# A chunk's gate, output projection and residual addition one slot later in a pipelined Mamba-2 and mixture-of-experts block

## The chip, the core and the metric

The kernel runs on one core of a Trainium2 chip. Its time is the device time of one execution in microseconds. Five engines with queues of their own work side by side: PE (matrix products; its weight loads are listed as PEld), DVE, ACT and POOL (elementwise work), and SP, which here only issues DMAs. Each queue runs in order, so an instruction that waits holds up all that stand behind it on its engine.

## The reference

Eight sequences of 512 tokens with 128 features go through a modulated layer norm, four Mamba-2 layers with a residual, a gated residual, and a mixture of eight experts (two per token) with a shared expert. The change lies in the Mamba layers. The reference steps through the tokens one by one; cut to what matters:

```
for l in range(4):
    zxbcdt = rmsnorm(h) @ Wi                      # z, xBC, dt
    xBC = silu(conv4(xBC)); xs, Bm, Cm = split(xBC)
    dt  = softplus(dt + dtb); dA = exp(-dt * exp(Alog))
    hs  = hs * dA_t + (dt_t * xs_t) B_t           # per token t, per head
    y_t = hs . C_t + D * xs_t
    h   = h + rmsnorm(y * silu(z), gw) @ Wo
```

## The kernel before

The recurrence is done in chunks of 128 tokens. A unit is one sequence in one layer; there are 32 units (u), of four chunks each, so 128 chunks, called items (i). Two units form a group, whose running sums are made together. Everything is float32.

One Python loop (L993) runs over slots t, and each slot takes a different stage of several items, so that the stages form a software pipeline. The context manual_schedule keeps the written order on every engine. The order in a slot sets the order of the queues; what makes an engine wait is data or a buffer. For the code, p = t + 16 is the slot of the projections, whose units are four ahead.

In a slot t, in this order:

- ACT takes the exponent of item t+1's decay matrix dV (decay_exp, L809).
- PE makes item t's part from the state and the state's increment (state_out, L861 and L870, into a bank py) and item t-1's output (chunk_out, L910 and L920, into its py).
- POOL scales the state (state_decay, L886) and weighs the transposed input (weigh, L836 and L839).
- In every fourth slot ACT does silu of z and of the convolution's output (L672, L673), into a tile sz for z.
- DVE multiplies dV by the Gram matrix (mix, L852), in even slots adds the finished pair of items t-4 and t-3 into the residual (out_add, L967), and finishes the state (state_next, L895 and L902; for a first chunk ACT copies it, L900).
- DVE multiplies item t-1's output by silu(z) (gate, L932) and ACT squares it (square, L936).
- PE makes the group's running sums in every eighth slot (sums_a, L748 to L750), then projects item t-2 (project_out: L947 sums the squares, L951 is the product with Wo). Two items share one bank po, in which an even one starts a new tile.
- PE makes item t+1's Gram matrix (gram, L848) and item t+2's transposes (L828), which ACT copies to xT (L830). Both go into one bank, ptx, the only one of its pool.
- POOL subtracts and masks item t+2's decay (L793, L798). DVE does three convolution taps (L660) and, between them in odd slots, the scale of the pair (out_scale: L958 on DVE, the power at L959 on POOL).
- The generators of gens take one step each. renorm, one per unit, normalizes a finished unit for the next layer: squares on ACT (L155), a power on POOL (L150), scaling on ACT (hn, L203), a slot with nothing, transposes on PE and the copy hT on ACT (L208, L210). At the end of the stage rejoin does the same for the mixture's input.
- PE projects dt (L682), DVE does one piece of softplus (L706 to L740), DVE and ACT copy out the running sums (sums_b, L756 to L763), SP writes them to DRAM as crow (L765) and POOL makes dtd (L767) of them. PE projects one part of x (px, L638) and ACT starts its convolution (L650); in every fourth slot PE projects z (pz, L644). SP loads item t+4's decay rows from crow into dV (L779).

The parts of a slot recur after eight slots. With r = t modulo 8: sums_a and sums_b are in r3; silu is in r1 and r5, z in r0 and r4; renorm starts in r3 and r7 and ends four slots later, in the slot in which the next one starts.

The pools that matter: psY (py, two banks), psO (po, two), psX (ptx, one), psP (all other products, three banks), eight in all; szp (sz, four tiles, L576); wk (g and sq, two each). scale_weights (L604, L605) puts four operations on POOL at the head of one slot r4 in 32 slots.

Of the kernel before, what the change touches and what calls it, by code (L numbers as in the profile page):

```python
# [13 lines left out]
PSUM = bass.MemoryType.PSUM  # L14
# [6 lines left out]
LEAD = 4  # L21
# [3 lines left out]
def adaln_mamba_moe(  # L25
# [28 lines left out]
    B, L, DM = x.shape  # L54
# [4 lines left out]
    NC = L // Q  # L59
# [445 lines left out]
    def pbank(name):  # L505
        return psP.tile([P, 512], F32, tag="p", name=name)
# [66 lines left out]
    with ExitStack() as actx:  # L573
# [7 lines left out]
        df = actx.enter_context(tc.tile_pool(name="df", bufs=6))  # L581
        rows = actx.enter_context(tc.tile_pool(name="rows", bufs=3, space=bass.MemoryType.DRAM))
        psX = actx.enter_context(tc.tile_pool(name="psX", bufs=1, space=PSUM))
        psY = actx.enter_context(tc.tile_pool(name="psY", bufs=2, space=PSUM))
        psO = actx.enter_context(tc.tile_pool(name="psO", bufs=2, space=PSUM))

        U = NL * B
        NI = U * NC
# [6 lines left out]
        def load_weights(l):  # L595
            Wi[l] = wip.tile([P, NPROJ], F32, tag="Wi", name=f"Wi{l}")
            nc.sync.dma_start(Wi[l], W_in[l])
            Wo[l] = wp.tile([P, NB, DM], F32, tag="Wo", name=f"Wo{l}")
            nc.sync.dma_start(Wo[l], W_out[l].rearrange("(k p) m -> p k m", p=P))
# [27 lines left out]
        def renorm(u):  # L627

            l, b = divmod(u, B)
            yield from rms_transposed(b, 1e-5, bw[:, l + 1 : l + 2], f"_{u}", pbank, htp, NC - 2)  # L630
            hT[u + B] = hTs.pop(b)
# [8 lines left out]
        def project_z(v):  # L640
            l = v // B
            for k in range(NB):
                pz[v, k] = pbank(f"pz{v}_{k}")
                nc.tensor.matmul(pz[v, k][:, :L], Wi[l][:, k * P : (k + 1) * P], hT[v], start=True, stop=True)  # L644
# [124 lines left out]
        def where(i):  # L769

            u, s = divmod(i, NC)
            g, bi = divmod(u, GROUP)
            return u, s, g, bi * n + s * NH
# [37 lines left out]
        def item_slice(i):  # L811
            s = i % NC
            return slice(s * Q, (s + 1) * Q)
# [115 lines left out]
        def gate(i):  # L929
            u, s, g, h0 = where(i)  # L930
            gs[i] = wk.tile([P, NB, Q], F32, tag="g", name=f"g{i}")
            nc.vector.tensor_mul(gs[i], py.pop(i)[:, :NB, :], sz[u][:, :, item_slice(i)])  # L932

        def square(i):
            sqs[i] = wk.tile([P, NB, Q], F32, tag="sq", name=f"sq{i}")
            nc.scalar.activation(sqs[i], gs[i], AF.Square)  # L936


        def project_out(i):
            l = i // NC // B  # L940
            g, sq = gs.pop(i), sqs.pop(i)
            c = i % 2
            if c == 0:
                po[i // 2] = psO.tile([P, 512], F32, tag="o", name=f"po{i}")
            pp = po[i // 2]
            for k in range(NB):
                nc.tensor.matmul(  # L947
                    pp[:, 2 * DM + c : 2 * DM + c + 1], sq[:, k, :], ones[:, 0:1], start=(k == 0), stop=(k == NB - 1)
                )
            for k in range(NB):  # L950
                nc.tensor.matmul(  # L951
                    pp[:, c * DM : (c + 1) * DM], g[:, k, :], Wo[l][:, k, :], start=(k == 0), stop=(k == NB - 1)
                )

        def out_scale(i):
            if i % 2:
                rs = small.tile([P, 2], F32, tag="rg", name=f"rg{i}")
                nc.vector.tensor_scalar(rs, po[i // 2][:, 2 * DM : 2 * DM + 2], 1.0 / DI, 1e-5, ALU.mult, ALU.add)  # L958
                nc.gpsimd.tensor_tensor(rs, rs, mhalf[:, 0:2], ALU.pow)  # L959
                po[i // 2] = po[i // 2], rs  # L960

        def out_add(i):
            if i % 2:
                pp, rs = po.pop(i // 2)
                for c in range(2):
                    b, s = i // NC % B, i % NC - 1 + c
                    nc.vector.scalar_tensor_tensor(  # L967
                        hs[b][:, s, :], pp[:, c * DM : (c + 1) * DM], rs[:, c : c + 1], hs[b][:, s, :], ALU.mult, ALU.add
                    )

        def item(i):
            return 0 <= i < NI

        def unit(v):
            return 0 <= v < U

        def group_stages(p, stages):

            for stage, late in stages:
                q, r = divmod(p - late, NC)  # L980
                if r == 0 and unit(q) and q % GROUP == GROUP - 1:
                    stage(q // GROUP)

        actx.enter_context(tc.manual_schedule())
        gens = {}
# [4 lines left out]
                    del gens[key]  # L990

        EARLY = 9
        for t in range(-NC * LEAD - EARLY, NI + 4):  # L993
            p = t + NC * LEAD
            drain = p >= NI
            if p == 5 - EARLY:
                gens["small"] = load_small()
            if p == 0:
                gens["experts"] = prepare_experts(df)
            if p == 7 - EARLY:  # L1000
                gens["lists"] = clear_lists()
            if t == NI - LEAD * NC + 2:
                for k, w in enumerate((sw1, sw2.rearrange("(k p) o -> p k o", p=P))):
                    w12.append(wip.tile([P, NPROJ], F32, tag="Wi", name=f"ws{k}")[:, :FH])
                    dst = w12[k] if k == 0 else w12[k].rearrange("p (k o) -> p k o", o=DM)
                    nc.sync.dma_start(dst, w)
            for g, seqs in enumerate(sets):
                if t == NC * (U - B) + NC * (seqs[-1] + 1) + 2:
                    gens["pairs", g] = rejoin(g)
            v, j = divmod(p, NC)  # L1010
            vc, jc = divmod(p - 1, NC)

            if (p + 2 * NC) % (NC * B) == 0 and unit(p // NC + 2):
                load_weights((p // NC + 2) // B)
            if p % (NC * B) == NC and unit(v):
                scale_weights(v // B)
            if p == NC:
                nc.scalar.activation(negA, negA, AF.Exp)
                nc.scalar.mul(negA, negA, -1.0)
            if (p + EARLY) % NC == 0 and 0 <= (p + EARLY) // NC < B:  # L1020
                gens[(p + EARLY) // NC] = enter((p + EARLY) // NC)
            if t % NC == 3 and unit(t // NC - 1) and t // NC - 1 + B < U:
                gens[t // NC - 1 + B] = renorm(t // NC - 1)

            if item(t + 1):
                decay_exp(t + 1)

            if item(t):
                state_out(t)
            if item(t - 1):  # L1030
                chunk_out(t - 1)
            if item(t):
                state_decay(t)
            if item(t + 1):
                weigh(t + 1)
            if drain and scatters and item(t + 2):
                scatter(*scatters.pop(0)[1:])
            vz, jz = divmod(p - 5, NC)
            if jz == 0 and unit(vz):
                silu(vz)  # L1040
            if item(t):
                mix(t)
            if item(t - 3):
                out_add(t - 3)
            if item(t):
                state_next(t)
            if drain:
                step_pairs()
            if item(t - 1):
                gate(t - 1)  # L1050
                square(t - 1)
            group_stages(p, ((sums_a, 7),))
            if item(t - 2):
                project_out(t - 2)
            if item(t + 1):
                gram(t + 1)
            if item(t + 2):
                transposes(t + 2)
            if item(t + 2):
                decay_diff(t + 2)  # L1060
                decay_mask(t + 2)
            if unit(vc):
                conv_tap(vc, jc, 1)
            if item(t - 2):
                out_scale(t - 2)
            if unit(vc):
                conv_tap(vc, jc, 2)
                conv_tap(vc, jc, 3)
                px.pop((vc, jc))
            for key in list(gens):  # L1070
                if not step(gens[key]):
                    del gens[key]
            if drain and routed:
                serve()
            if j == 1 and unit(v):
                project_dt(v)
            group_stages(p, ((softplus_a, 2), (softplus_b, 3), (softplus_c, 5), (softplus_d, 6), (sums_b, 7)))
            if unit(v):
                project_x(v, j)
                conv_first(v, j)  # L1080
            if j == 0 and unit(v - 1):
                project_z(v - 1)
            if item(t + 4):
                decay_rows(t + 4)

# [244 lines left out]
```

## Time and profile before

| | us |
|---|---|
| median of 3 runs (lowest, highest) | 1151.76 (1150.76, 1159.22) |
| the profiled execution, its span | 1149.48, 1147.8 |
| PE busy | 967.3 (84%) |
| DVE busy | 855.8 (75%) |
| ACT busy | 763.3 (67%) |
| POOL busy | 856.6 (75%) |
| first and last mix (L852) | 88.35, 859.67 |
| mean granted PE clock | 0.925 |

The page's second part cuts the span into 40 slices and gives the busy tenths of each:

```profile
PE   2767899889999999999988999979564994999985
DVE  2768888798888978988879889988754652666653
ACT  3686889789798788787978988776624741333320
POOL 6877979789798897887988988889766163555550
```

One character is 28.7 us. The even middle, characters 4 to 27, is the pipelined stage of the Mamba layers; then come its end with the routing, and the experts, where PE is at nine tenths. The change touches the stage up to about 880 us alone.

Busy time is an engine's own account; a wait is told by who ended it. "ACT sq L936 <- DVE g L932" means that ACT stood idle ahead of the instruction that writes sq at L936, until DVE's at L932 was done.

### The profile page before, as it was taken

The page shows a single profiled execution, that of the slowest core. Times are in us where ns is not written, and L with a number is a line of the kernel's source. Part 1 is how long each engine was busy: PE and PEld are TensorE (multiplying, and loading weights), DVE is VectorE, ACT ScalarE, POOL GpSimd, SP SyncE. Part 2 cuts the span into 40 slices and gives each one's busy share as a digit, 9 for nine tenths or more (in the row PEclk, how much of TensorE's full clock was granted, in tenths as well). Part 3 has the DMA queues.
Part 4 walks back from the last instruction along what each step waited for, and adds up shares of the span by engine and source line. Part 5 has one row for each costly group of instructions (what it writes and reads, how often), then busy time and mean ns, then how long its engine had stood idle before and what let it go on. Part 6 is the DMA issues. An engine that isn't in the chain of part 4 may idle for free. (4 is left out here: it accounts for less than half of the span.)

```text
span 1147.8 us, 21568 instructions
## 1 busy us (share of the span) xinstructions
PE 967.3 (84%) x7130; PEld 736.7 (64%) x7130; DVE 855.8 (75%) x2084; ACT 763.3 (67%) x1641; POOL 856.6 (75%) x937
## 2 busy tenths in 40 slices
PE   2767899889999999999988999979564994999985
PEld 1335667666776667676766776667453673889972
DVE  2768888798888978988879889988754652666653
ACT  3686889789798788787978988776624741333320
POOL 6877979789798897887988988889766163555550
PEclk8688999899999999999999999977886897999997
DMA  6954736425234243242332433424201015878746
GB/s 161 238 156 147 215 106 202 121 81 158 84 132 127 76 143 102 86 157 90 127 109 71 159 108 107 154 89 150 72 22 38 7 44 157 228 219 231 229 143 224
DMA packets 134303, 151.21 MB, mean 132 GB/s; under 512 B 22568, under 2 KB 106696, under 8 KB 134192
## 3 DMA queue, kind: packets, MB, share of 16 engines
q1 hardware_dynamic: 127184, 137.91, 40.1%
q0 software_dynamic: 4672, 9.42, 2.5%
q10 hardware_dynamic: 2336, 2.50, 0.7%
q8 instruction: 57, 0.93, 0.3%
q14 instruction: 54, 0.44, 0.1%
HBM read 120.07 MB, written 29.71 MB: 130 GB/s over the span
## 5 line engine op out<-in xcount | busy, mean ns | idle before, releaser
L660 DVE SCALAR_TENSOR_TENSOR xbc<-px,cw,xbc 128x511 f32<-128x511 f32 (+2 forms) x384 | 285.9, 745 | 20.7 <-ACT xbc L650 13.6
L793 POOL TENSOR_TENSOR dV<-dV,cum 128x1024 f32<-128x1024 f32 x128 | 244.3, 1909 | 1.5 <-DMA dV<-crow 1.4
L852 DVE TENSOR_TENSOR dV<-dV,ptx 128x1024 f32<-128x1024 f32 x128 | 154.9, 1210 | 12.7 <-ACT xT L830 12.6
L809 ACT ACTIVATE dV<-dV 128x1024 f32<-128x1024 f32 x128 | 134.6, 1051 | 32.8 <-POOL dV L798 32.5
L798 POOL TENSOR_SCALAR_AFFINE_SELECT dV<-dV 128x1024 f32<-128x1024 f32 x128 | 141.9, 1109 | 9.3
L488 POOL DMA_INDIRECT yg<-y,ix x78 | 84.1, 1079 | 77.7 <-DVE y L1216 63.0
L638 PE MATMUL px<-hT,Wi 128*128 128x512 f32 x192 | 107.6, 644 | 22.9 <-ACT hT L210 11.7
L650 ACT ACTIVATE xbc<-px,cbias,cw 128x512 f32<-128x512 f32 x128 | 98.9, 773 | 36.1 <-PE px L638 34.9
L936 ACT ACTIVATE sq<-g 128x256 f32<-128x256 f32 x128 | 53.1, 414 | 79.0 <-DVE g L932 71.2
L488 POOL DMA_INDIRECT xg<-row,ix x64 | 63.6, 993 | 50.6 <-ACT unread L313 25.7
L836 POOL TENSOR_TENSOR xd<-xT,dt 128x256 f32<-128x256 f32 x128 | 79.3, 619 | 28.5 <-ACT xT L830 28.5
L861 PEld LDWEIGHTS py<-xbc,st 128*128 128x128 f32 x384 | 62.4, 207 | 55.8 <-issue 45.0
L951 PE MATMUL po<-Wo,g 128*128 128x128 f32 x512 | 89.9, 299 | 0.0
L1198 ACT ACTIVATE hd<-ph,bs 128x256 f32<-128x256 f32 x78 | 32.8, 471 | 83.7 <-PE ph L1192 83.7
L910 PEld LDWEIGHTS py<-xbc,dg 128*128 128x128 f32 x512 | 81.4, 206 | 7.6 <-issue 1.0
L920 PE MATMUL py<-dV,xd 128*32 128x128 f32 x2048 | 85.8, 287 | 0.0
L947 PEld LDWEIGHTS po<-ones,sq 128*128 128x128 f32 x512 | 68.2, 194 | 26.0 <-issue 18.1
L910 PE MATMUL py<-xbc,dg 128*128 128x128 f32 x512 | 83.3, 288 | 0.0
L947 PE MATMUL po<-ones,sq 128*128 128x1 f32 x512 | 78.7, 258 | 0.4 <-ACT sq L936 0.4
L1205 PE MATMUL pe<-w,hd 128*128 128x128 f32 x624 | 75.9, 275 | 0.0
L1192 PE MATMUL ph<-xt,w 128*128 128x256 f32 x312 | 75.8, 387 | 0.0
L1205 PEld LDWEIGHTS pe<-w,hd 128*128 128x128 f32 x624 | 72.7, 192 | 0.1
(252 smaller groups left out, 2326.8 us busy)
## 6 DMA issues: line engine op xcount, KB each, us to landing
dV<-crow SPq DMA_DIRECT2D x128, 512.0 KB
w<-in_L_ffn_ew_dram SPq DMA_DIRECT2D x78, 256.0 KB
xg<-blank SPq DMA_DIRECT2D x64, 260.0 KB
ecum<-crow SPq DMA_DIRECT2D x256, 48.0 KB
rows<-xg SPq DMA_DIRECT2D x39, 130.0 KB
b<-in_L_ffn_eb_dram SPq DMA_DIRECT2D x39, 64.0 KB
x<-in_L_attn_x_dram SPq DMA_DIRECT2D x8, 256.0 KB
md<-mods SPq DMA_DIRECT2D x8, 256.0 KB
```

What stands on the lines that cost most here:

```text
L488: i = nc.gpsimd.indirect_dma_start(out=to, out_offset=bass.IndirectOffsetOnAxis(ap=ix, axis=0), in_=of, in_offset=None)
L638: nc.tensor.matmul(px[v, k][:, :L], Wi[l][:, c0 : c0 + P], hT[v], start=True, stop=True)
L650: nc.scalar.activation(xbc[v][:, k, :], px[v, k][:, :L], AF.Identity, bias=cbias[:, l, k : k + 1], scale=cw[:, l, k, KT - 1 : KT],)
L660: nc.vector.scalar_tensor_tensor(xbc[v][:, k, d:], px[v, k][:, : L - d], cw[:, l, k, KT - 1 - d : KT - d], xbc[v][:, k, d:], ALU.mult, ALU ...
L793: nc.gpsimd.tensor_tensor(dV[i], dV[i], cums[g][:, h0 : h0 + NH].unsqueeze(2).to_broadcast([P, NH, Q]), ALU.subtract)
L798: nc.gpsimd.affine_select(out=dV[i], in_=dV[i], pattern=[[0, NH], [1, Q]], compare_op=ALU.is_ge, fill=-200.0, base=0, channel_multiplier=-1,)
L809: nc.scalar.activation(dV[i], dV[i], AF.Exp)
L852: nc.vector.tensor_mul(Ms[i], Ms[i], pg.pop(i).unsqueeze(1).to_broadcast([P, NH, Q]))
L910: nc.tensor.matmul(py[i][:, k, :], dg[l][:, k, :], xbc[u][:, k, t], start=False, stop=True, skip_group_check=True,)
L947: nc.tensor.matmul(pp[:, 2 * DM + c : 2 * DM + c + 1], sq[:, k, :], ones[:, 0:1], start=(k == 0), stop=(k == NB - 1))
L951: nc.tensor.matmul(pp[:, c * DM : (c + 1) * DM], g[:, k, :], Wo[l][:, k, :], start=(k == 0), stop=(k == NB - 1))
L1205: nc.tensor.matmul(pe[:, s, :], hd[:, k, s * P : (s + 1) * P], w2[:, k, :], start=(k == 0), stop=(k == FK - 1))
```

## The change

gate, square, project_out, out_scale, out_add and the start of renorm come one slot later, each in the place in the slot that it had. So gate follows chunk_out of its item by a slot, out_add falls into odd slots, out_scale into even ones, and renorm starts in r0 and r4. rejoin starts one slot later and the loop runs one slot longer. psY gets three banks and psO one, eight in all as before. sums_a goes from the middle of r3 to its end, behind the projections of x; sums_b goes from the end of r3 to the middle of r4, behind gate and square. No instruction is added or taken away.

```diff
-        psY = actx.enter_context(tc.tile_pool(name="psY", bufs=2, space=PSUM))
-        psO = actx.enter_context(tc.tile_pool(name="psO", bufs=2, space=PSUM))
+        psY = actx.enter_context(tc.tile_pool(name="psY", bufs=3, space=PSUM))
+        psO = actx.enter_context(tc.tile_pool(name="psO", bufs=1, space=PSUM))
...
-        for t in range(-NC * LEAD - EARLY, NI + 4):
+        for t in range(-NC * LEAD - EARLY, NI + 5):
...
-                if t == NC * (U - B) + NC * (seqs[-1] + 1) + 2:
+                if t == NC * (U - B) + NC * (seqs[-1] + 1) + 3:
                     gens["pairs", g] = rejoin(g)
...
-            if t % NC == 3 and unit(t // NC - 1) and t // NC - 1 + B < U:
-                gens[t // NC - 1 + B] = renorm(t // NC - 1)
+            if t % NC == 0 and unit(t // NC - 2) and t // NC - 2 + B < U:
+                gens[t // NC - 2 + B] = renorm(t // NC - 2)
...
             if item(t):
                 mix(t)
-            if item(t - 3):
-                out_add(t - 3)
+            if item(t - 4):
+                out_add(t - 4)
             if item(t):
                 state_next(t)
             if drain:
                 step_pairs()
-            if item(t - 1):
-                gate(t - 1)
-                square(t - 1)
-            group_stages(p, ((sums_a, 7),))
             if item(t - 2):
-                project_out(t - 2)
+                gate(t - 2)
+                square(t - 2)
+            group_stages(p, ((sums_b, 8),))
+            if item(t - 3):
+                project_out(t - 3)
...
-            if item(t - 2):
-                out_scale(t - 2)
+            if item(t - 3):
+                out_scale(t - 3)
...
-            group_stages(p, ((softplus_a, 2), (softplus_b, 3), (softplus_c, 5), (softplus_d, 6), (sums_b, 7)))
+            group_stages(p, ((softplus_a, 2), (softplus_b, 3), (softplus_c, 5), (softplus_d, 6)))
             if unit(v):
                 project_x(v, j)
                 conv_first(v, j)
             if j == 0 and unit(v - 1):
                 project_z(v - 1)
+            group_stages(p, ((sums_a, 7),))
             if item(t + 4):
                 decay_rows(t + 4)
```

## The prediction

> **What bounds the kernel now.** I read the page's slices first: from 100 to 780 us all four engines are busy in eight or nine tenths and the pattern repeats, so the pipelined stage is 680 of 1147.8 us. Then one period of it, eight slots, from the start of one mix (L852) to that of the same slot of the next group. I call a slot r0 to r7 by t modulo 8. The busy time of that stretch (columns: span, then busy time and count of PE, PEld, DVE, ACT, POOL, clock, DMA share, GB/s):
>
> ```profile
> 421.02:466.29 45.27, 42.30 (x373) 32.24 (x371) 39.82 (x85) 39.38 (x79) 39.15 (x43) 1.00 0.39 113
> ```
>
> No engine is full: four of them carry 39 to 42 us of 45.27. What remains is waiting on one another, so I took the waits of 150 to 750 us (engine, line, releaser: total, times, longest), some 13 periods:
>
> ```profile
> ACT sq L936 <- DVE g L932: 45.4, 32, 5.4
> POOL dtd L767 <- ACT edec L763: 38.9, 13, 4.2
> DVE py L895 <- PE py L870: 29.4, 27, 1.3
> ...
> DVE st L902 <- POOL st L886: 12.8, 12, 2.8
> ...
> DVE g L932 <- PE py L920: 11.3, 17, 3.3
> PE pc L748 <- DVE dt L740: 10.8, 13, 0.9
> ...
> DVE dV L852 <- ACT xT L830: 10.4, 12, 0.9
> ```
>
> The two long ones are ACT's and POOL's; what sets the pace is read on DVE, whose own waits are four short ones. Its timeline, starts of r3, r4, r5 and r6 with the waits between (start, duration, in brackets the idle time before and its releaser):
>
> ```profile
> 439.03 1.21 DVE L852 TENSOR_TENSOR dV<-dV,ptx 128x1024 f32<-128x1024 f32 x1
> ...
> 443.44 1.21 DVE L852 TENSOR_TENSOR dV<-dV,ptx 128x1024 f32<-128x1024 f32 x1
> ...
> 445.62 0.42 DVE L932 TENSOR_TENSOR g<-py,sz 128x256 f32<-128x256 f32 x1 [0.45 <-PE py L920]
> ...
> 448.19 1.21 DVE L852 TENSOR_TENSOR dV<-dV,ptx 128x1024 f32<-128x1024 f32 x1
> 450.68 0.43 DVE L895 TENSOR_TENSOR py<-py,ecum 128x256 f32<-128x256 f32 x1 [1.29 <-PE py L870]
> 451.55 0.42 DVE L902 TENSOR_TENSOR st<-st,py 128x256 f32<-128x256 f32 x1 [0.43 <-POOL st L886]
> ...
> 455.55 1.22 DVE L852 TENSOR_TENSOR dV<-dV,ptx 128x1024 f32<-128x1024 f32 x1 [0.93 <-ACT xT L830]
> ```
>
> The slots of this period last 4.20, 7.16, 6.65, 4.41, 4.75, 7.36, 5.08, 5.66 us (r0 to r7); DVE stalls only in r1 (1.03), r4 (0.45) and r5 (2.65 to the next mix). The last of these comes from ACT, whose timeline ahead of that mix is gapless:
>
> ```profile
> 449.70 1.06 ACT L809 ACTIVATE dV<-dV 128x1024 f32<-128x1024 f32 x1 [0.83 <-POOL dV L798]
> 450.77 1.28 ACT L672 ACT_TABLE_LOAD   x1
> 452.07 1.09 ACT L672 ACTIVATE sz<-pz 128x512 f32<-128x512 f32 x2
> 453.04 1.92 ACT L673 ACTIVATE xbc<-xbc 128x2048 f32<-128x2048 f32 x1
> 454.84 0.42 ACT L936 ACTIVATE sq<-g 128x256 f32<-128x256 f32 x1
> 455.15 0.37 ACT L830 COPY xT<-ptx 128x256 f32<-128x256 f32 x1
> ```
>
> Followed back: that exp waited for POOL's mask, this for dtd (L767, 445.17), this for the group's running sums on ACT, behind renorm's squares, behind xT, behind PE's sums_a, which waited 0.92 us for DVE's dt (438.90). So the group's sums close the loop once per period.
>
> **What the Trainium skill says.** "Perfetto Trace Analysis", Optimization Strategy: the same gap in every period can mean too few buffers for the next tile. The trace agrees in part: 0.09 to 0.45 us ahead of gate is a true data wait, not a buffer. "PSUM — Partial Sum Buffer", PSUM bank collisions: any two engines on one bank must be ordered, reads too. It agrees: the mix waited 0.93 us for a copy (xT) out of another part of its bank. This matters for one output bank. "ScalarE: Activation LUTs", What ACT_TABLE_LOAD costs: 1283 ns plus a drain of some 1380. The row has 1.28 us and the silu 1.30 us after the load's start, so no drain shows; I use 1.30.
>
> **The change part by part.** Nothing is added to any engine; everything moves. The removed waits are gate's (0.45 + 0.09 us in this period; 11.3 us over 13 periods, 0.9 on average) and sums_a's 0.92. Durations below are from start to start in the four engines' timelines of this period. Moved work by slot: out_add (0.52, 433.51 to 434.03) from even to odd slots, out_scale (0.12) from odd to even; the two DVE copies of sums_b (0.40, 443.04 to 443.44) from r3 to r4; renorm's transposes (PE 0.47), hT copy and squares (ACT 0.59 and 1.60) from r3 and r7 to r4 and r0, its scaling (four hn, 1.2) from r1 and r5 to r2 and r6, its rsqrt (POOL 1.25) to r1 and r5.
>
> *r3 to r5.* With one bank, project_out of an even chunk, always in an odd slot, must wait until out_add has read the pair before, which DVE runs in that slot after mix. From the mix of r3 as zero: out_add ends at 1.73 (as in r2: 432.38 to 434.11) and PE goes on at 1.77: project_out, gram, transposes (1.55), px (0.86), sums_a (0.92): 5.10; in r4 state product and chunk_out (1.54), project_out (1.00): 7.64, gram and transposes: xT can start on ACT at 8.39. Then hT at +0.38, squares, conv_first, exp at 0.38 + 0.59 + 1.60 + 0.66 = +3.23: 11.62, and from exp to the next mix 5.85 as in the rows above: r6 starts at **17.47**; before, 16.52. So **+0.95**. On DVE the same stretch ends at 16.0: PE has renorm's transposes, px and pz (0.47 + 0.86 + 1.93) and the state product (1.08) after 8.19, which reaches DVE at 12.53, then 3.5 of work. Hidden by that 1.4: out_scale in r4 waiting some 0.8 for project_out, and out_add in r5 waiting some 0.6 for POOL's power behind dtd and mask. Without this cover they would cost 1.4.
>
> *r6, r7.* 4.68 + 6.06, before 5.08 + 5.66: nothing. *r0, r1:* mix ends, PE gram and transposes: xT at 1.27 + 0.75 = 2.02, exp at 5.25, next mix at 11.10; before 11.36: **-0.26** (DVE alone 10.84: its work of 3.80 + 6.33 and 0.7 for PE's state product). *r2:* out_add leaves: **-0.40**. Sum +0.29 a period; 13 regular ones, +4.
>
> *dtd.* It waits on POOL ahead of decay_diff now, not behind mask, until ACT has edec, by my count at 7.0 from r3's mix; diff and mask end at 10.3 and the exp that needs them starts at 11.62. Hidden by the ACT chain; if that were short, dtd would be next. In three periods scale_weights (four POOL operations, 397.54 to 399.87) stood behind the late dtd and made r5 last 9.72 us instead of 7.36. Now they come ahead of the wait, which covers them: **3 x -2.3 = -7**.
>
> *DMAs.* On SP's queue crow's write comes after one more dV load and only half a slot ahead of the load that reads it. The write's issue moves from 5.83 to some 6.9 after r3's mix; 2.84 us later (444.86 to 447.70) the load can go, at 9.8, and POOL wants it near 19. Costs nothing; with less than 9 us of cover it would.
>
> *sz.* Its four buffers (L576) are not widened. silu of unit v runs in slot 4v-11 and takes the buffer of unit v-4, whose last gate moves from slot 4v-12 into 4v-11 itself. So silu on ACT gets a wait for a DVE gate which stands behind state_next, thus behind PE. By my times gate ends at 13.8 (r5) and 7.4 (r1, from r0), silu starts at 14.0 and 7.6: hidden by 0.2 only. No row shows this wait. Its lower bound is nothing, a gain being excluded; its upper one 1.1 us in each, if ACT's table load stands behind the wait (13.8 + 1.30 + 3.48 = 18.6 for 17.5). I take nothing, since the load is an instruction of its own ahead of silu.
>
> *End.* The loop gets one slot more, and rejoin of the last pair starts one later. The slots there last up to 14 us (859.67 is the last mix, 880.88 the last out_add), but DVE idles 7.8 us ahead of that out_add for POOL's power behind eleven scatters. From -3 to +8; I take +3.
>
> Sum: 4 - 7 + 3 = 0. The profiled execution took 1149.48 us (span 1147.8), 2.3 below the median of 1151.76, so I forecast the median, **1152 us**.
>
> **The rivals.** *A, as summed*: a tie, 0.42. *B, faster*: PE is not held in r3 (the bank comes free earlier than I think, or PE's lead absorbs it), so r4 and r5 go like r0 and r1: 11.1 plus 0.5 for the sums, 16.0 from r3 instead of 16.52. A period is 1.2 shorter; 13 x -1.2 - 7 + 3 = -19: 1133 us. For it: PE stood idle 0.92 us in r3 before and has much lead there; against it: out_add and the bank are in the code. If all coupling fell away, DVE's 41.1 us (the period less its three stalls) would be the floor, 13 x -4.1: 1098, which the ACT chain speaks against. Chance 0.35. *C, slower*: silu's wait for gate comes ahead of the table load: 2 x 1.1 us a period over 13 periods, 29 us: 1181. It decides as soon as gate ends after ACT's exp, and by my count it does in both silu slots. Against it: the load is separate. Chance 0.15. *D, not what it says*: gate is freed, but DVE then stops at out_scale or out_add for the same PE and POOL work, and these stalls aren't covered: 1.4 a period less the gains above, 18 - 4: 1166. Chance 0.08.
>
> **How the numbers follow.** About 1% (11.5 us) is what a measurement can tell from no change. A gives same 0.30, faster 0.07, slower 0.05; B faster 0.29, same 0.06; C slower 0.15; D slower 0.06, same 0.02: faster 0.36, same 0.38, slower 0.26. A's own range is 1141 to 1163. For 8 in 10 I reach below B's value by 4 and to 1176, leaving out most of C and B's tail.
>
> **What would show it.** Right: gate's wait for PE gone; PE waiting for h (L967) ahead of po in r3 and r7; ACT gapless from xT in r4 to xT in r5; dtd's wait shorter than 2.8 us; r5 no longer 9.7 with scale_weights. Wrong: r3 to r6 under 16 us (B); an idle ACT ahead of its table load with gate as releaser (C); DVE waits at L958 or L967 that sum above 1 us a period (D). A DVE that never waits would overturn all of it.

## The result, and the profile after

| | before | after |
|---|---|---|
| median of 4 runs (lowest, highest), us | 1155.49 (1150.76, 1165.57) | 1204.99 (1202.08, 1208.76) |
| profiled execution's span, us | 1147.8 | 1204.8 |
| mean granted PE clock | 0.925 | 0.912 |

After to before is **1.042** (95% interval 1.034 to 1.050): slower by 4%, where 1152 us had been forecast and 1176 was the upper end of the range. The slices of the page, to be laid beside those of before, with the clock below them:

```profile
PE   3758888889888898988988888886776794999995
...
DVE  2868878887787877878878887886874643656653
ACT  3767878777786776877878777756653651333320
POOL 6876978978687796877988878768885254555550
PEclk8889989999898898989999999987777796999998
```

Where before had nines and eights there are mostly eights and sevens, on all four engines at once, from character 4 to 27. So no engine has become the bound; all of them wait more. The first mix is at 90.41 us, that of t=112 at 791.40. Measured from t=8 to t=112, which is 13 periods, the stage has grown from 604.5 to 649.5 us: 45.0 of the 57.0 us between the spans. Another 10.3 lie after t=112 and 1.7 ahead of t=8.

The 13 periods are not alike. Here are two of the change, each from an r0 to the next (columns as in the row of before: span, then busy time and count of PE, PEld, DVE, ACT and POOL, clock, DMA share, GB/s):

```profile
495.70:546.60 50.90, 44.43 (x331) 33.47 (x331) 40.26 (x85) 36.80 (x76) 38.53 (x43) 0.90 0.35 111
599.15:647.10 47.95, 41.49 (x353) 31.38 (x352) 40.06 (x85) 38.35 (x77) 41.86 (x48) 1.00 0.32 106
```

The second ran at full clock and still takes 47.95 us where before took 45.27. The first takes three more, with a mean clock of 0.90. These look like two different losses, and the waits between 150 and 750 us name a candidate for each (total, times, longest):

```profile
PE po L947 <- DVE h L967: 49.5, 23, 3.0
...
ACT sq L936 <- DVE g L932: 34.9, 20, 2.2
POOL dtd L767 <- ACT edec L763: 34.0, 12, 3.6
...
ACT L672 <- DVE g L932: 28.8, 24, 2.7
DVE dV L852 <- ACT xT L830: 27.3, 29, 1.5
...
DVE v L687 <- PE pdt L682: 22.0, 24, 1.2
...
DVE rg L958 <- PE po L951: 18.8, 17, 2.0
```

Gate's wait for PE (11.3 us before) has left the list, which the change was to remove. Three waits are new to it: PE for out_add ahead of the one output bank, ACT for gate at L672, and DVE for project_out at L958.

**The wait at L672** is small in the list but sits on the chain. ACT between the xT copies of r4 and r5, where no wait stood ahead of the table load before, and the gate on DVE in the same microseconds:

```profile
525.63 0.48 ACT L830 COPY xT<-ptx 128x384 f32<-128x384 f32 x1 [1.40 <-PE ptx L828]
...
528.92 1.04 ACT L809 ACTIVATE dV<-dV 128x1024 f32<-128x1024 f32 x1
531.08 1.28 ACT L672 ACT_TABLE_LOAD   x1 [1.12 <-DVE g L932]
532.38 1.09 ACT L672 ACTIVATE sz<-pz 128x512 f32<-128x512 f32 x2
...
535.45 0.37 ACT L830 COPY xT<-ptx 128x256 f32<-128x256 f32 x1
...
530.58 0.42 DVE L932 TENSOR_TENSOR g<-py,sz 128x256 f32<-128x256 f32 x1
```

The idle 1.12 us stands ahead of the *table load*, whose row names no tile. It ended when DVE had done the gate, at 531.00. Silu needs the tile sz that this gate frees; its wait is carried out before the load, so the load is not done meanwhile. It occurs 24 times, mostly 1.12 us each, in both silu slots.

**The wait at L947** on PE, in r3 of the same period:

```profile
512.45 0.64 PE L920 MATMUL py<-dV,xd 128*32 128x128 f32 x16
516.08 0.99 PE L947 MATMUL po<-ones,sq 128*128 128x1 f32 x4 [2.98 <-DVE h L967]
516.92 1.20 PE L951 MATMUL po<-Wo,g 128*128 128x128 f32 x4
...
518.98 1.91 PE L638 MATMUL px<-hT,Wi 128*128 128x512 f32 x2
```

The mix of r3 began at 514.20, so PE went on 1.88 us after it; 1.77 was predicted. But what follows runs slowly: the product px, which is listed as two instructions, takes 1.91 us, and 1.02 in a kernel shown below. The windows of these microseconds say why (columns as above; the clock is the third number from the end):

```profile
511.00:514.00 3.00, 2.09 (x26) 1.43 (x24) 2.79 (x10) 3.00 (x9) 3.00 (x5) 1.00 0.32 113
514.00:516.00 2.00, 0.00 (x0) 0.00 (x0) 2.00 (x6) 0.52 (x1) 1.93 (x2) 0.87 0.00 0
516.00:519.40 3.40, 3.32 (x14) 3.28 (x15) 2.75 (x5) 0.59 (x2) 0.57 (x1) 0.50 0.00 0
519.40:522.80 3.40, 3.40 (x11) 1.95 (x10) 2.02 (x5) 2.03 (x3) 1.19 (x2) 0.57 0.00 0
522.80:526.00 3.20, 3.20 (x39) 2.88 (x38) 1.53 (x4) 1.62 (x7) 1.69 (x2) 1.00 0.12 24
```

The records of the clock show half of it from 515.50 on, while PE still waits, for 6.8 us. So PE is late for r4 too: DVE waits 1.64 us for project_out at L958, and xT of r4 starts 11.43 us after the mix of r3, where 8.39 was counted.

So far this is a reading of traces. The experiments take the two waits away, one at a time.

### The profile page after: what moved, and what is told of

Its sections match the earlier page's. It is cut to its first block, busy times and chain, and to the rows that moved or that the text cites. A ratio compares the mean times of both kernels' runs of the same rounds, so it can differ in the third digit from the quotient of the medians.

```text
span 1204.8 us, 21565 instructions
## 1 busy us (share of the span) xinstructions
PE 984.0 (82%) x7130; PEld 750.5 (62%) x7130; DVE 865.6 (72%) x2084; ACT 761.8 (63%) x1641; POOL 855.9 (71%) x937
## 4 chain that ended last, share of the span: by engine, by line
PE 34%; DVE 27%; ACT 14%; POOL 10%; DMA 7%; issue 5%; SPq 2%; POOLq 0%; DVEq 0%; ACTq 0%
DVE xbc L660 7%; DVE dV L852 6%; PE px L638 4%; PE pe L1206 4%; PE pz L644 4%; ACT xbc L673 4%; DMA rows<-xg 3%; PE ph L1193 3%; POOL xg L488 3%; ACT L672 3%; POOL dV L793 2%; ACT sz L672 2%; DVE py L895 2%; PE py L870 2%; PE po L951 2%
## 5 line engine op out<-in xcount | busy, mean ns | idle before, releaser
L947 PE MATMUL po<-ones,sq 128*128 128x1 f32 x512 | 80.8, 262 | 73.2 <-DVE h L967 62.6
L947 PEld LDWEIGHTS po<-ones,sq 128*128 128x128 f32 x512 | 71.6, 202 | 100.6 <-issue 67.3
L830 ACT COPY xT<-ptx 128x384 f32<-128x384 f32 (+1 forms) x128 | 57.2, 447 | 66.1 <-PE ptx L828 65.0
L951 PE MATMUL po<-Wo,g 128*128 128x128 f32 x512 | 95.8, 313 | 0.0
```

Of the source, the lines that this page charges most:

```text
L947: nc.tensor.matmul(pp[:, 2 * DM + c : 2 * DM + c + 1], sq[:, k, :], ones[:, 0:1], start=(k == 0), stop=(k == NB - 1))
L951: nc.tensor.matmul(pp[:, c * DM : (c + 1) * DM], g[:, k, :], Wo[l][:, k, :], start=(k == 0), stop=(k == NB - 1))
```

## The experiments

Each ratio is to the kernel before on the same chip. In the last four rows that kernel took 1173 to 1174 us, elsewhere 1154 to 1155, so times are compared within a row only. "Period" is the mean of the 13 periods from t=8 to t=112, "half rate" the time in that stretch for which the trace records the PE clock below 0.9.

| kernel | period, us | half rate, us | ratio (95% interval) |
|---|---|---|---|
| before | 46.50 | 32.2 | 1 |
| the change | 49.96 | 64.9 | 1.042 (1.034, 1.050) |
| fifth sz tile | 47.87 | 63.5 | 1.020 (1.017, 1.022) |
| out_add at the slot's end | 51.0 | 109.2 | 1.061 (1.058, 1.063) |
| both of these | 46.22 | 44.4 | 1.004 (1.002, 1.005) |
| before, sums moved | 46.13 | 14.5 | 0.997 (0.995, 0.999) |
| gate first, two banks each | 50.85 | 78.5 | 1.054 (1.047, 1.061) |
| before, renorm later | 46.54 | 41.0 | 1.000 (0.998, 1.002) |
| fifth sz, renorm back | 47.69 | 46.3 | 1.013 (1.010, 1.017) |
| fifth sz, out_add first | 46.46 | 49.4 | 0.997 (0.995, 0.999) |
| fifth sz, out_add first in r3 and r7 | 46.53 | 46.1 | 0.995 (0.991, 0.998) |
| the same, renorm back | 47.82 | 71.7 | 1.011 (1.006, 1.016) |
| fifth sz, PE's wait filled | 45.91 | 3.4 | 0.992 (0.990, 0.995) |
| the change, PE's wait filled | 48.34 | 13.7 | 1.020 (1.013, 1.028) |

### Silu's wait: a fifth tile for sz

```diff
-szp = actx.enter_context(tc.tile_pool(name="szp", bufs=4))
+szp = actx.enter_context(tc.tile_pool(name="szp", bufs=5))
-df = actx.enter_context(tc.tile_pool(name="df", bufs=6))
+df = actx.enter_context(tc.tile_pool(name="df", bufs=5))
```

The memory for the fifth tile comes from the pool of dV (df).

> The changed kernel with a fifth sz tile (and five dV tiles for six, to make room). Theory S, silu's wait for gate ahead of ACT's table load costs its own 1.12 us twice a period: that wait is gone, some 28 us come back, about 1176 us. Theory B, PE held for out_add by the one output bank sets the pace and silu's wait lies in its shadow: the idle time moves to another ACT wait, 1195 us or more. If five dV tiles are too few, POOL waits for DMA at decay_diff.

Measured: 1177.3 us beside 1153.73. ACT's waits between 150 and 750 us in this kernel, all of them down to 2.7 us:

```profile
ACT xT L830 <- PE ptx L828: 51.8, 43, 2.2
ACT sq L936 <- DVE g L932: 37.2, 21, 2.5
ACT xbc L650 <- PE px L638: 19.2, 27, 1.2
ACT st L900 <- PE py L870: 2.7, 5, 0.7
```

L672 is gone, and with it half of the loss. Its periods at full clock take 45.75 us; those of the change take 47.95; the difference, 2.20, is twice the 1.12 us of one wait within 0.04. So the 28.8 us in the list went into the time nearly one for one, as theory S said. The dV tile that was given up shows no cost: waits for dV's rows come to 1.1 us, in the change to 1.5. PE's wait for out_add is still there, and so is the half rate:

```profile
PE po L947 <- DVE h L967: 46.2, 24, 2.5
```

### The one output bank: where out_add stands

First out_add one slot sooner, behind the convolution's taps, so that the bank is free before the next slot's project_out comes to it. Once with four and once with five tiles for sz:

```diff
             if item(t):
                 mix(t)
-            if item(t - 4):
-                out_add(t - 4)
...
                 px.pop((vc, jc))
+            if item(t - 3):
+                out_add(t - 3)
```

> The changed kernel with out_add moved from behind the next slot's mix to behind the convolution taps of the slot of out_scale, so that the one output bank is free before project_out asks for it. Theory B: PE's wait for h (49.5 us between 150 and 750 us) falls below 10 us, the clock stays full, 25 to 35 us come back: 1170 to 1180 us. Theory S: most of the loss is ACT's wait for gate, which stays: 1195 us or more. DVE may wait for POOL's power at the end of r4 instead, up to 1.7 us a period, 22 us: then hardly a gain.

> Both edits, fifth sz tile and out_add at the end of its slot. If the two waits are all that the change lost: 1140 to 1155 us. If the moved work itself (renorm's squares and hT copy ahead of silu, running sums ahead of decay_diff) costs time: 1165 us or more.

Measured: 1225.58 us with four tiles, slower than the change itself; 1158.2 with five, between the two ranges that were expected (PE's wait for h falls from 46.2 to 10.0 us). The same move costs some 20 us in one surrounding and saves 19 in the other. DVE's waits of the kernel with four tiles, and ACT's at L672:

```profile
ACT L672 <- DVE g L932: 43.6, 23, 2.5
...
DVE h L967 <- POOL rg L959: 30.1, 12, 2.7
```

In r4, out_add now stops DVE for up to 2.7 us until POOL has made the power, behind its late work on the decay. The gates behind it are late in turn, and silu with its table load waits for a gate: 43.6 us instead of 28.8. With a fifth tile silu does not wait for that gate. By this reading, a wait that DVE can hide is passed on through sz when sz is short; so the two losses are not independent of what is moved.

Then out_add ahead of mix, with five tiles:

```diff
+            if item(t - 4):
+                out_add(t - 4)
             if item(t):
                 mix(t)
-            if item(t - 4):
-                out_add(t - 4)
```

> The fifth-sz kernel with out_add ahead of mix in the same odd slot. PE's wait for h in r3 shrinks by a mix (1.13 us), from 2.5 to 1.4 us, and in r7 to nothing; if it is the long idle that halves PE's clock, the half-rate time falls from 64 us to below 45 and the time to 1155 to 1168 us. If only the wait's own length counts: two times 1.1 us less a period at most where PE sets the pace, about 1165 us, with the half-rate time unchanged. DVE then waits for POOL's power in r5 ahead of mix, which may eat half a microsecond a period.

Measured: 0.997 (1153.5 us), below both ranges. PE's wait and DVE's at out_add in this kernel:

```profile
DVE h L967 <- POOL rg L959: 33.9, 19, 3.1
...
PE po L947 <- DVE h L967: 27.4, 21, 2.4
```

PE's wait falls by 19 us, in r3 from 2.51 to 1.38 us, and yet the half rate comes in every period, mostly for 3.4 us. DVE pays with 33.9 us for POOL's power. Doing it in r3 and r7 alone, the slots in which PE waited:

> The fifth-sz kernel with out_add ahead of mix in r3 and r7 alone, where PE is early, and behind mix in r1 and r5, where DVE waited up to 2.2 us for POOL's power with it ahead. If that wait is real time, the stage loses it: r4 and r5 together 11.5 to 12.5 us for 13.0, 1125 to 1145 us. If ACT's chain from xT in r4 to xT in r5 sets that stretch anyway, as the prediction counted: no change, 1148 to 1158 us.

Measured: 0.995 (0.991 to 0.998), which is the second reading, no change. DVE's wait for the power drops to 20.9 us, and the period does not follow (46.53). The difference to the run before is within the intervals.

### The parts of the change alone

The sums moved, in the kernel before:

```diff
-            group_stages(p, ((sums_a, 7),))
+            group_stages(p, ((sums_b, 8),))
...
-            group_stages(p, (... (softplus_d, 6), (sums_b, 7)))
+            group_stages(p, (... (softplus_d, 6)))
...
                 project_z(v - 1)
+            group_stages(p, ((sums_a, 7),))
```

> The kernel before with only sums_a at the end of its slot and sums_b in the middle of the next. If this part is good by itself, as the prediction's count has it (scale_weights covered, no PE wait of 0.92 us for dt): 1138 to 1148 us, and r5 with scale_weights no longer than the other r5. If dtd ahead of decay_diff makes POOL late: 1160 us or more.

renorm's start from r3 and r7 to r0 and r4, in the kernel before:

> The kernel before with renorm alone starting one slot later. By the prediction's count ACT gets 2.2 us ahead of silu in r0 and r4 and loses 1.2 us behind it: r0 and r1 together 11.1 to 11.7 us (before 11.36), r4 and r5 some 12 to 13: within 1% of the kernel before. If this moved work is what is left of the loss after both waits are gone: 1160 to 1170 us.

The reverse, renorm back in the changed kernel, with five tiles for sz, and in the kernel with out_add first in r3 and r7:

> The fifth-sz kernel with renorm back at its old slot (r3 and r7). If the one output bank alone made the 1177 us of that kernel: no change, 1170 to 1184 us, PE's wait for h still 2.5 us in r3. If it is renorm's work ahead of silu: 1150 to 1162 us.

> The same with renorm back in r3 and r7, which takes hT copy and squares (2.2 us of ACT) out of that chain. If the chain is what is left: 10 to 25 us faster than with renorm late, below 1140 us. If DVE, PE and POOL bind in turn: within 6 us of it.

Measured: 0.997 for the sums (1150.41 us, between the two ranges), 1.000 for renorm later. Moving renorm back gave 1.013 beside 1.020 in one surrounding (1172.45 us, in the range of the first reading) and 1.011 beside 0.995 in the other (21 us slower, which neither reading had). So neither part carries the loss, and what renorm's place is worth has no fixed sign here; the half rate went from 63.5 to 46.3 us in the first pair and from 46.1 to 71.7 in the second, the same way as the time.

A period of the sums-only kernel at full clock takes 45.77 us, half a microsecond *more* than before (45.27). Its small gain comes from two other things: r5 lasts 7.9 us in the periods with scale_weights too, where before had 7.36 and three times 9.72, and the half rate is 14.5 us instead of 32.2. With five tiles the whole change takes 45.75: so the rest of the change, the later gate in it, together added nothing to a period at full clock, and took nothing from it.

Last, whether the third bank for py is needed: gate and square ahead of mix, with two banks for py and two for po.

```diff
-        psY = actx.enter_context(tc.tile_pool(name="psY", bufs=3, space=PSUM))
-        psO = actx.enter_context(tc.tile_pool(name="psO", bufs=1, space=PSUM))
+        psY = actx.enter_context(tc.tile_pool(name="psY", bufs=2, space=PSUM))
+        psO = actx.enter_context(tc.tile_pool(name="psO", bufs=2, space=PSUM))
...
+            if item(t - 2):
+                gate(t - 2)
+                square(t - 2)
             if item(t):
                 mix(t)
...
-            if item(t - 2):
-                gate(t - 2)
-                square(t - 2)
             group_stages(p, ((sums_b, 8),))
```

> The changed kernel with gate and square ahead of mix in the slot. Then py needs two banks again and po gets two, and sz stays at four tiles. Silu's wait ends before it starts (gate stands at the head of DVE's slot) and project_out has a free bank. If the two waits made the loss, both must go without any sixth of memory: ACT's wait ahead of its table load and PE's for h near zero, half-rate clock in the stage near that of the kernel before (32 us), 1140 to 1156 us. If the moved renorm or the one slot more at the end costs much by itself: 1160 us or more.

Measured: 1215.34 us, which is above 1160, but the trace shows another cause than those that were named for it. PE's waits for gate, from the list of 150 to 750 us:

```profile
PE py L861 <- DVE g L932: 48.2, 33, 2.3
...
PE py L870 <- DVE g L932: 21.7, 11, 2.0
```

ACT's wait at L672 is gone without a fifth tile, since gate comes earlier, but PE now waits 70 us for it at the head of the slot. With the bank taken back, PE's wait moves from the output to the state product and grows from 49.5 us to 70. The place of gate and the banks changed together here, so their shares are not told apart.

### The clock: PE's wait filled with work

With the fifth tile, PE's wait remains and so does its half rate. Which of them costs? In the next kernels PE makes eight products more per period, into a half of py that nobody reads any more, ahead of the wait: once with five tiles and once with four.

```diff
         def chunk_out(i):
...
+            if i % 4 == 2:
+                for _ in range(5 if i % 8 == 2 else 3):
+                    nc.tensor.matmul(py[i][:, NB:, :], xbc[u][:, NB + 1, t], xbc[u][:, :NB, t],
+                                     start=True, stop=True, skip_group_check=True)
```

> Five tiles for sz and, at the end of chunk_out in the slots r3 and r7 alone, five and three more matrix products of 128x128 by 128x256 (0.40 us each in the row of L870 at full clock, so 2.0 and 1.2 us) into the dead half of the bank py, whose result nobody reads. They fill the time in which PE waited for out_add (46.2 us in 24 waits between 150 and 750 us with five tiles and no fill). Theory (the wait itself is covered, and what costs is the clock that halves after PE has stood idle): half-rate time between t=0 and t=120 falls from 63.5 us to under 25, the mean period from 47.87 to about 45.7, and the ratio to the kernel before from 1.020 to 0.995, though PE does 3.2 us more work a period. Rival (the wait itself is the loss, clock or no clock): the ratio stays at 1.02 or rises, the period stays at 47.9 or more, since the products come on top where they overrun the wait.

> The change with its four tiles for sz, plus the same filling products in r3 and r7. Theory (two losses that add up: silu's wait for gate 28 us, and the clock some 26 us): half-rate time falls from 64.9 us to under 30, the waits of ACT for gate ahead of its table load stay at 1.1 us each, mean period from 49.96 to about 48.0 (the periods of the change that had no half-rate time), ratio from 1.042 to about 1.02. Rival (the wait itself is the loss): ratio 1.04 or more. Third: PE's filled time makes chunk outputs and gates later and so silu's wait longer than 1.1 us: ratio between 1.02 and 1.04 with the wait at 1.5 us or more.

Measured: 0.992 with five tiles and 1.020 with four, close to what the theory said in both; the rival wanted 1.02 or more and 1.04 or more. (The half-rate times in these two texts, 63.5 and 64.9 us, are those of the table, from t=8 to t=112.) PE in r3 of the kernel with five tiles; its line numbers from L929 on are ten higher, so that L930 is the filling, listed as two instructions for each product, and L957 the start of project_out:

```profile
479.39 2.42 PE L930 MATMUL py<-xbc 128*128 128x256 f32 x10
481.98 0.58 PE L957 MATMUL po<-ones,sq 128*128 128x1 f32 x4 [0.16 <-DVE h L977]
...
483.49 1.02 PE L638 MATMUL px<-hT,Wi 128*128 128x512 f32 x2
```

The mix of r3 began at 480.10, so project_out goes on 1.88 us after it, as in the change: the hold is as long. But the product px behind it takes 1.02 us, not 1.91. A period of this kernel, from r0:

```profile
462.71:508.46 45.75, 44.84 (x371) 34.26 (x370) 39.87 (x85) 38.39 (x78) 39.47 (x44) 1.00 0.40 123
```

PE is busy 44.84 of 45.75 us, and the period is no longer than the full-clock ones without the filling. Eleven of the 13 periods take 45.74 to 45.76. So the wait for the bank was covered, as the prediction said, and what it cost was the clock. In the kernel with four tiles the wait at L672 (gate is L942 there) is untouched by the filling, and nine of its periods take 47.95 to 48.23:

```profile
ACT L672 <- DVE g L942: 28.8, 24, 2.7
```

Set beside each other, the change has 1.042, with the fifth tile alone 1.020, with the filling alone 1.020, with both 0.992. The filling took 21 us off the stage with four tiles (649.5 to 628.4 us from t=8 to t=112) and 25 with five (622.3 to 596.9).

## Why the prediction was wrong

**The size of the loss.** The span grew by 57.0 us. By the terms of the prediction's sum, with one row for what it left out, from the periods at full clock (45.27 before, 47.95 after, 45.75 with five tiles) and the sums of all 13 (604.5 and 649.5):

| term | predicted, us | measured, us |
|---|---|---|
| the moved work, 13 periods | +4 | +6 (13 x 0.48) |
| scale_weights, three periods | -7 | -7 (3 x 2.36) |
| silu's wait for sz | 0 | +29 (13 x 2.20) |
| what else the periods last beyond those at full clock | 0 | +17 (26 after, 9 before) |
| start and end | +3 | +12 (1.7 and 10.3) |
| sum | 0 | +57 |

**The step that failed: "I take nothing, since the load is an instruction of its own ahead of silu."** The prediction had the bound, 1.1 us in each of two slots, and as rival C the sum, 29 us. It took the other end of the bound on an argument about the code. The trace shows the wait ahead of the load, 1.12 us, and the fifth tile shows that all of it was on the path. The count of when gate ends was good: 13.87 us after r3's mix in a period at full clock, for 13.8. But "hidden by 0.2 only" of silu's start was a lead far too short for a load of 1.28 us. The question to ask of such a lead is whether it is still enough if load and silu wait together. It was not.

**The term that was missing: the clock.** The prediction let PE wait in r3 and called it covered. The work was covered; the clock was not. The kernel before held the hint: its period was read from one stretch with a clock of 1.00 and 45.27 us, while the mean over 13 was 46.50, with 32.2 us at half rate. Eight of the 13 periods before had half-rate time and lasted 46.4 to 49.3 us, 16 us in all beyond 13 times 45.27. Three times 2.36 of them are no loss of the clock but scale_weights': ACT's exp, at full clock, waited 3.19 us for POOL's mask in such a period of before and 0.83 in the one that the prediction reads.

```profile
404.13 1.06 ACT L809 ACTIVATE dV<-dV 128x1024 f32<-128x1024 f32 x1 [3.19 <-POOL dV L798]
```

That leaves 9 us before and, as this delay is gone in the change, 26 after. The row of +17 is this difference. It is the clock's in the main and not to the microsecond, since the first and the last of the 13 periods can differ for other reasons as well (3 us of the 9, 5 of the 26); that filling PE's wait took off 21 and 25 us is the direct measure of what the clock costs these kernels.

The other steps, in their order:

- *Gate's wait for PE gone*: right. No such line is left in the list.
- *r3 to r6 in 17.47 us, +0.95*: nearly right. With silu's wait and the half rate away, in the filled kernel with five tiles, it takes 17.62 us. The change itself takes between 18.7 and 21.8, so B's sign, under 16, never came.
- *r0 and r1 in 11.10*: 11.24 there, and 12.34 in the change's periods at full clock, which is one silu wait more. *r6 and r7 as before*: 10.74 both.
- *PE would wait for h in r3 and r7*: right, 2.98 and 1.39 us.
- *dtd's wait shorter than 2.8*: no, 34.0 us in 12 waits, 2.8 each. But between 150 and 750 us no exp of the change waits for POOL's mask any more (before: 17.2 us in 13 waits), so it cost nothing there, as said.
- *r5 no longer 9.7 with scale_weights*: right. r5 takes 9.26 in the change in periods with it and without it, one silu wait in it, and 8.16 in the filled kernel with five tiles.
- *DVE waits at L958 or L967 above 1 us a period would show D*: they came (26.5 us in all, 2 a period), and D is still not the cause: the filled kernel with five tiles has 22.6 us of them and a period of 45.75. That sign was badly chosen, since these waits were the ones said to be covered; their sizes, some 0.8 and 0.6, were good (0.82 and 0.54 to 0.81).
- *The end, +3 with -3 to +8*: measured +10.3 after t=112, and +4.4 with five tiles. The last two silu waits of the change are 7.4 us together; 4.5 of the 10.3 come in the experts, which the change does not touch, and stay unexplained.

The chances put 0.15 on the rival that carries the largest part of the loss, and 0.42 on the tie.

A small gain over before is to be had (0.992), but it is not shown to be the later gate's: at full clock a period of that kernel is half a microsecond longer than before, and the time comes from scale_weights (7 us) and the half rate (3.4 us for 32.2). Whether filling PE's idle time in the kernel before gives as much was not tried.

## What to carry to other kernels

When a step of a software pipeline moves one slot later, list every pool that it reads, not only those that the change widens: each tile lives a slot longer, and the pool that was not widened is where the next wait comes. When all that hides a wait is the work of the very instruction that has to wait, or of the load put ahead of it, count it as not hidden until a trace shows otherwise. And a wait on PE that is covered in the schedule can still cost: read the granted clock of the period, and compare the period that you price with the mean of all.

## What the runs showed of the hardware

**An activation's wait stands ahead of its table load.** 24 times ACT stood idle ahead of a 1.28 us load whose row names no tile, since the activation behind it waited for a buffer. The Trainium skill ("ScalarE: Activation LUTs", What ACT_TABLE_LOAD costs) gives 1283 ns for the load, and the trace agrees (1283 in every one of this kernel's). The further drain of some 1380 ns that it gives is not seen here: silu starts 1.29 us after its load's start, in all but two of the 448 cases in the fourteen traces.

**PE's clock halved after idle times of 1.4 us, and it mattered when they came.** The skill ("TensorE: Matmul & The Clock Gate", Why this matters for your kernels) asks for no idle gap of PE above some 3 us; here shorter ones were enough. With the fifth tile every drop between t=8 and t=112 followed an idle time of 1.36 to 2.52 us, in the change most followed 1.39 or 2.98. Half rate lasts 3.41 or 6.83 us at a time there, and all of it in the change begins on one grid of 3.41 us (262.9, 286.8, 310.7, 361.9 lie 7, 7 and 15 steps apart). The same page (The HAM clock gate) tells of a window of 3413 ns that runs freely, which agrees.

Laid on that grid, the change's waits sort without an exception. Of the twelve of 2.98 us in r3, the five that began 0.80 to 1.51 us after a grid point were followed by 6.8 us of half rate, the five at 1.62 to 1.95 by none, and the two at 1.96 and 2.12 by 3.4 us, one grid point later. Of the twelve of 1.39 us in r7, the four at 1.10 to 1.52 were followed by 3.4 us and the eight at 1.60 to 2.93 by none. That fits the three full-clock periods in a row of 47.95 us: 14 steps take 47.79, so the wait moved on the grid by only 0.16 us a period, from 1.62 to 1.95. What else counts is open: in the kernel before, two of the eight drops came with no idle time of PE longer than 0.46 us in the 3.4 us ahead of them.
